# Splitting 192 channels as 128 and twice 64, and moving ACT's copies a piece behind their matmuls, in a two-layer vision-Mamba kernel

## The chip, the cores and the metric

The kernel runs on one core of a Trainium2 chip. The metric is the device time of one execution in microseconds, the median of three runs. A core has the engines PE (matmuls), DVE (vector), ACT (scalar, activation tables), POOL (GpSimd) and SP, which here issues the DMAs. [...]

## The reference, cut to what matters

The input is 8 images of 64 x 64 pixels with 192 channels. Two layers follow each other. Per image, with L = 4096 pixels:

```python
# layer 0
xl, z = split(x @ W_in.T)                      # 192 -> 2 * 384
xc = silu(depthwise3x3(xl) + conv_b)
# two orders of the pixels (rows, columns), each with its own B, C (32 states) and dt (6 heads)
h = exp(dt * A) * h + (dt * x_t) B_t           # per head: 64 x 32
y = h C_t + D * x_t                            # the two orders are added
out = x + (y * silu(z)) @ W_out.T              # 384 -> 192
x1 = out + silu(out @ W1.T + b1) @ W2.T + b2   # 192 -> 768 -> 192
# layer 1, on x1
left  = relu(conv1x1(relu(bn(conv3x3(relu(bn(conv3x3(bn(x1[:96]))))))))
right = layernorm, projection to 192, depthwise conv, silu, then
        delta = softplus(dt_proj(dts) + bias)  # four directions, 192 channels
        h = exp(delta * A) * h + delta * u * B # 16 states per channel
        y = h C + D * u
        layernorm, times silu(z), projection to 96
out = shuffle(left, right) + x1
```

All of it is in f32 except the spreading of delta * u, which is done in three bf16 terms.

## The kernel before

**The spine** is `selective_scan`, layer 1's recurrence. Its work for 8 images is cut into 3072 units q, 384 per image: a unit has 8 channels times 16 states on 128 partitions and 1024 pixels. A tile is 16 units; it takes its delta and delta * u from `prepare`. Per unit, `fetch` brings delta by a DMA (4 units ahead), ACT's `decay` makes exp(delta * A) of it (L1322), PE's `spread` (L1330) lays delta * u over the states into one of two PSUM tiles dB, DVE multiplies by B (`weigh`, L1345) and scans (L1352), POOL multiplies by C (L1356), ACT's `carry_on` takes the last column (L1362, L1363), and every fourth unit PE's `gather` (L1374) sums over the states of four units into a PSUM tile acc, which ACT copies out (L1378). The gather runs two units behind the scan.

**The side work** is everything else: generators, one after the other, that the class `Beside` runs in pieces. For image b + 1 these are layer 0's `conv0` (projection to 384 and depthwise convolution), `ssd` (layer 0's recurrence, in 32 chunks of 128 pixels) and `mlp0` (gate, projection, and the two-layer product), then layer 1's `conv_branch` (with `scan_sums` aside) and `scan_outputs` of an earlier image, and `scan_inputs` and `transposed`, which make the next image's u. For the first image they run alone, before the scan begins, and in this first run the yields of each generator are added up as its cost.

The order of the work is set by this bookkeeping, not by a scheduler: all instructions are recorded in program order (`pin`). Each unit has two half slots. In a half slot the order is: the next piece of a running gather; then `Beside.half()`; then a piece of `prepare`; and in the first half `carry_on` of the unit before, `spread` of the next, and the scan. `half()` adds a rate to a credit and runs side pieces until the yields that they give have used it up; a `yield None` ends the half at once:

```python
        self.rate = (own + sum(self.costs.get(gen.__name__, 40.0) for gen in self.stages)) / halves
...
        self.credit = min(self.credit, self.rate) + self.rate
        while self.credit > 0.0 and self.stages:
            for cost in self.stages[0]:
                if cost is None:
                    return
                self.credit -= cost
                if self.credit <= 0.0:
                    return
```

`own` (465 before) stands for the scan's own PE work, which takes credit by `beside.spend`. In the last but one tile of an image, 23 units ahead of its end, `beside.finish()` runs at once whatever side work is left; then the next image's u is loaded and the next stages are started. `conv_branch` counts 190 and `scan_outputs` 78 as cost.

**Layer 0's matmuls before.** The 192 input channels lie on 96 partitions, twice. A product from 192 channels is two matmuls of 96 rows that add up: L362 in conv0 (512 columns), L693 (gate) and L739 (expand) in mlp0 (256 columns). A product to 192 channels makes two halves of 96 output partitions: L726 (project) and L757 (contract), 256 columns. mlp0 goes through 16 blocks of 256 pixels by stages that overlap by `in_turn` (L682 is the addition of the two orders on POOL). One f32 matmul shows as two rows in the trace, and L-numbers of a helper's matmul are those of the helper's line.

**ssd's chunk.** `in_turn` runs fetch, decays, weigh, outputs and store, a chunk apart, the oldest first. `decays` loads X by four DMAs, transposes B and C (L545), which ACT copies (bc, L549), and makes the decay factors M: PE's L555 and L556 into ps_d, ACT's exp (L557). `weigh` has POOL's xw (L571), dtx (L577) and the decayed state Hm (L579). `outputs` has the state sums on PE (L589), DVE's additions to Hm (L595) and Hn (L611), POOL's Hn (L597), and the outputs (L605, L620, L626) with DVE's additions (L615, L633). `store` writes y by four DMAs.

Outside dB's two, PSUM has four tiles of 512 columns during the scan; `cx.one` hands them out for all side work, for the gather and for `prepare`. `prepare` makes delta's raw values by two matmuls of 12 rows, one per half of the pixels (L1262), each followed by ACT's work on its half.

Of the kernel before, what the change touches and what calls it, by code (L numbers as in the profile page):

```python
# [41 lines left out]
NXP = 4 * NS + 2 * RK  # L42
# [66 lines left out]
def setup(cx, cp, dp, p0, p1):  # L109
# [42 lines left out]
    k["b2"] = const(p0["b2"].rearrange("(a p) -> p a", p=CH), [CH, 2], "b2")  # L152
# [34 lines left out]
    nc.sync.dma_start(out=k["dtw"][4 * NS : NXP], in_=p1["dtw"].rearrange("g r t m -> r g t m"))  # L187
# [138 lines left out]

def conv0(cx, x):
# [3 lines left out]
    with cx.pool("cw0") as wp, cx.pool("v0", 2) as vp:  # L331
        w_in = wp.tile([CH, 2, INNER0], F32, tag="w_in", name="w_in")
        pin(nc.sync.dma_start(out=w_in, in_=k["p0_w_in"].rearrange("(a p) m -> p a m", p=CH)[:, :, :INNER0]))
# [11 lines left out]
        first = vp.tile([CH, 2, R2 * WW], F32, tag="xt", name="first")[:, :, :WW]  # L345
        pin(nc.sync.dma_start(out=first, in_=x[:, 0:WW].rearrange("(a p) l -> p a l", p=CH)))
        xts, xcs = {}, {}

        def load(p):

            n = min(R2, HH - 1 - p * R2)
            xts[p] = vp.tile([CH, 2, R2 * WW], F32, tag="xt", name="xt")
            at = (p * R2 + 1) * WW
            pin(nc.sync.dma_start(
                out=xts[p][:, :, : n * WW], in_=x[:, at : at + n * WW].rearrange("(a p) l -> p a l", p=CH)
            ))

        def rows_in(j, src, n, at):

            ps = cx.one("ps_in")  # L360
            for a in range(2):
                pin(nc.tensor.matmul(  # L362
                    ps[:, : n * WW], lhsT=w_in[:, a, j * 128 : (j + 1) * 128], rhs=src[:, a, :], start=a == 0, stop=a == 1
                ))
            pin(nc.scalar.copy(
                pads[j][:, at : at + n, 1 : 1 + WW], ps[:, : n * WW].rearrange("p (h w) -> p h w", w=WW)
            ))

        def project(p, j):
            pad = pads[j]  # L370
            if p == 0:
                rows_in(j, first, 1, 1)
            else:
                pin(nc.gpsimd.tensor_copy(pad[:, 0:2, :], pad[:, R2 : R2 + 2, :]))
            for b in range(2):
                n = min(RB, HH - 1 - p * R2 - b * RB)
                if n < RB:
                    pin(nc.gpsimd.memset(pad[:, R2 + 1, :], 0.0))
                rows_in(j, xts[p][:, :, b * RB * WW : (b * RB + n) * WW], n, 2 + b * RB)
                yield 2.4  # L380
# [58 lines left out]
def ssd(cx):  # L439
# [15 lines left out]
    with cx.pool("g0", 2) as gp, cx.pool("s0", 2) as sp:  # L455
# [79 lines left out]
        def decays(c):  # L535
# [3 lines left out]
            for d in range(2):  # L539
                for i, (at, dims) in enumerate(token_rows(k["xrows"], d, c, 1)):  # L540
                    src = bass.AP(k["xrows"].tensor, k["xrows"].offset + at, [dims[0], [1, INNER0]])
                    pin(nc.sync.dma_start(out=flat(X[chunks[i], d]), in_=src))
            ps = cx.one("ps_t")
            for i in range(2):
                pin(nc.tensor.transpose(  # L545
                    ps[: 2 * N0, i * Q : (i + 1) * Q], both[:, c % GC, i].rearrange("p d n -> p (d n)"), k["ident"]
                ))
            bc = sp.tile([2 * N0, 2, Q], F32, tag="bc", name="bc")
            pin(nc.scalar.copy(bc.rearrange("p i t -> p (i t)"), ps[: 2 * N0, : 2 * Q]))  # L549
            yield 0.6  # L550
            M = sp.tile([128, 2, NH, S], F32, tag="M", name="M")
            R = st[c].pop("R")
            for d in range(2):
# [3 lines left out]
                pin(nc.scalar.activation(flat(M[:, d]), ps, AF.Exp))  # L557
                yield 1.0
            st[c].update(X=X, bc=bc, M=M)

        def weigh(c):
# [7 lines left out]
            heads = "p d h c -> p (d h) c"  # L569
            xw = sp.tile([128, 2, NH, HP], F32, tag="xw", name="xw", bufs=1)  # L570
# [7 lines left out]
            Hm = sp.tile([2 * N0, NH, HP], F32, tag="H", name="Hm", bufs=4)  # L578
            pin(nc.gpsimd.tensor_mul(Hm, state[c], bcast(over[:, 0, c % GC, :], 2, HP)))  # L579
            st[c].update(dtx=dtx, xw=xw, Hm=Hm)  # L580

        def outputs(c):
# [26 lines left out]
            yield None  # L609
            ps = pss[1].rearrange("p (h c) -> p h c", c=HP)  # L610
            pin(nc.vector.tensor_add(Hn, ps, Hn))  # L611
            yo = sp.tile([128, 2, NH, HP], F32, tag="yo", name="yo")
# [23 lines left out]
        def store(c):  # L636
            yo = st.pop(c)["yo"]
            yield 0.0
            for d in range(2):
                y = k["yrows"][d]  # L640
                for i, (at, dims) in enumerate(token_rows(y, d, c, 1)):
                    dst = bass.AP(y.tensor, y.offset + at, [dims[0], [1, INNER0]])
                    pin(nc.sync.dma_start(out=dst, in_=flat(yo[chunks[i], d])))
            yield 0.0
# [4 lines left out]
def mlp0(cx, x, x1):  # L649

    nc, pin, k = cx.nc, cx.pin, cx.k
    NF, T = HID // 128, 256
    with cx.pool("mw0") as wp, cx.pool("m0", 2) as mp:
        def weight(n, shape, src):
            t = wp.tile(shape, F32, tag=n, name=n)
            pin(nc.sync.dma_start(out=t, in_=src))
            return t

        w_z = weight("w_z", [CH, 2, INNER0], k["p0_w_in"].rearrange("(a p) m -> p a m", p=CH)[:, :, INNER0:])
        w_out = weight("w_out", [128, NJ, C], k["p0_w_out"].rearrange("(j p) m -> p j m", p=128))  # L660
        w1 = weight("w1", [CH, 2, HID], k["p0_w1"].rearrange("(a p) m -> p a m", p=CH))
        w2 = weight("w2", [128, NF, C], k["p0_w2"].rearrange("(f p) m -> p f m", p=128))
        gT = wp.tile([128, NJ, T], F32, tag="gT", name="gT")
        h1 = wp.tile([128, NF, T], F32, tag="h1", name="h1")
        tiles = (slice(0, 2), slice(2, 3))
        st = {}

        def cols(i):
            return slice(i * T, (i + 1) * T)

        def load(i):
            st[i] = {}
            for d, bufs in ((0, 3), (1, 1)):
                t = st[i]["y", d] = mp.tile([128, 2, INNER0], F32, tag=f"y{d}", name=f"y{d}", bufs=bufs)
                pin(nc.sync.dma_start(out=t, in_=k["yrows"][d][cols(i)].rearrange("(q p) c -> p q c", p=128)))
            xt = st[i]["xt"] = mp.tile([CH, 2, T], F32, tag="xt", name="xt", bufs=4)
            pin(nc.sync.dma_start(out=xt, in_=x[:, cols(i)].rearrange("(a p) l -> p a l", p=CH)))
            yield 0.0

        def add(i):  # L680
            y0, y1 = st[i]["y", 0], st[i].pop(("y", 1))
            pin(nc.gpsimd.tensor_add(y0, y0, y1))  # L682
            yield 0.0

        def gate(i):
            xt = st[i]["xt"]
            zs = st[i]["zs"] = mp.tile([128, NJ, T], F32, tag="zs", name="zs", bufs=1)
            for js in tiles:
                ps = cx.one("ps_z")
                n = (js.stop - js.start) * T  # L690
                for j in range(js.start, js.stop):
                    for a in range(2):
                        pin(nc.tensor.matmul(  # L693
                            ps[:, (j - js.start) * T : (j - js.start + 1) * T], lhsT=w_z[:, a, j * 128 : (j + 1) * 128],
                            rhs=xt[:, a, :], start=a == 0, stop=a == 1,
                        ))
# [910 lines left out]
```

## Time and profile before

| | us |
|---|---|
| median of three runs | 18009.72 (18006.15 to 18019.03) |
| the profiled execution | 17986.38 |
| its span, first to last instruction | 17984.4 |
| PE, DVE, POOL, ACT busy | 14375.7, 12309.3, 12008.5, 10711.9 |
| mean granted PE clock | 0.815 of full |
| from the first scan to the last one's end | 980.8 to 17754.5 |

The span begins with 981 us in which the first image's layer 0 runs alone. Then come eight images of the scan, about 2190 us each in the steady state (less for the first and the last, which have less side work), and about 230 us of the last image's sums and outputs. The page's groups give each line's busy time, the mean of one instruction, and the time for which its engine stood idle before it with what ended that. A group's busy time counts rows that overlap once. The table of stretches gives, for chosen stretches of time, each engine's busy time, its instructions, the granted PE clock and the share of the DMA engines; the table for a line gives the same for that line's instructions alone.

### The profile page before, as it was taken

To read this page: it belongs to the slowest core of one execution; us is meant where nothing else is said; L and a number is where in the kernel's file an instruction comes from. 1 tells how busy PE (TensorE), PEld (TensorE's weight loads), DVE (VectorE), ACT (ScalarE), POOL (GpSimd) and SP (SyncE) were. 2 spreads that over 40 slices of the span, in tenths; PEclk is the share of its full clock that TensorE was granted. 3 is DMA by queue.
4 is the path that set the end of the run, shared out by engine and by line. 5 is a ranking of instruction groups with operands and counts; after the bars stand their busy time and mean duration, and the time that the engine had idled before them with its cause. 6 is when DMAs were issued, how large, how long until landed. Compare 5 with 4: busy or idle time off the path is not lost. (4 is left out here: it accounts for less than half of the span.)

```text
span 17984.4 us, 224777 instructions
## 1 busy us (share of the span) xinstructions
PE 14375.7 (80%) x76904; PEld 5676.6 (32%) x76904; DVE 12309.3 (68%) x9392; ACT 10711.9 (60%) x18482; POOL 12008.5 (67%) x6437
## 2 busy tenths in 40 slices
PE   8977788788877888778878788787888778868776
PEld 4623332343223431334313342233422334211111
DVE  2167787776667766677657775677766777667785
ACT  2464676466664756647566485664756557555654
POOL 3168776776668755687657875678755786657774
PEclk9987788789787887878878798787987779877676
DMA  3277777777677776777767777777776777677785
GB/s 85 75 201 177 189 190 202 168 193 199 170 195 174 192 194 164 196 176 201 186 170 188 176 199 185 184 188 178 197 183 178 184 183 198 180 194 190 184 196 143
DMA packets 1600969, 3238.93 MB, mean 180 GB/s; under 512 B 391580, under 2 KB 869396, under 8 KB 1596244
## 3 DMA queue, kind: packets, MB, share of 16 engines
q1 hardware_dynamic: 1599828, 3224.55, 71.2%
q8 instruction: 614, 10.06, 0.3%
q14 instruction: 527, 4.32, 0.1%
HBM read 2545.63 MB, written 678.18 MB: 179 GB/s over the span
## 5 line engine op out<-in xcount | busy, mean ns | idle before, releaser
L1356 POOL TENSOR_TENSOR h<-h,bc 128x1023 f32<-128x1023 f32 x3072 | 7223.5, 2354 | 3926.6 <-DVE h L1352 3412.2
L1352 DVE TENSOR_TENSOR_SCAN h<-dA,carry,dB 128x1024 f32<-128x1024 f32 x3072 | 7198.8, 2343 | 624.0 <-ACT dA L1322 188.7
L1345 DVE TENSOR_TENSOR dB<-dB,bc 128x1024 f32<-128x1024 f32 x3072 | 3741.5, 1218 | 2996.7 <-PE dB L1330 2948.1
L1322 ACT ACTIVATE dA<-dA,neg_a 128x1024 f32<-128x1024 f32 x3072 | 3486.8, 1135 | 797.5 <-DMA dA<-dld 795.3
L1374 PE MATMUL acc<-h,gather 128*32 128x512 f32 x12288 | 2479.9, 758 | 525.7 <-POOL h L1356 203.2
L1378 ACT COPY y<-acc 128x512 f32<-128x512 f32 x1536 | 886.5, 577 | 1908.7 <-PE acc L1374 1891.4
L1330 PE MATMUL dB<-dus,spread 24*128 24x512 bf16 x6144 | 1418.8, 430 | 365.3 <-DVE h L1352 283.8
L795 PE MATMUL ps_c<-p,conv_w 96*96 96x512 f32 x2304 | 1250.9, 670 | 120.5 <-ACT p L816 105.8
L1330 PEld LDWEIGHTS <-spread 24*128 24x128 bf16 x6144 | 317.6, 93 | 2607.9 <-issue 1700.3
L620 PE MATMUL ps_y<-dtx,M 64*64 64x64 f32 x12288 | 824.3, 267 | 393.5 <-DVE Hn L611 387.1
L1363 ACT ACTIVATE h<-h,bc 128x1 f32<-128x1 f32 x3072 | 905.1, 295 | 163.3 <-ACT carry L1362 3.8
L620 PEld LDWEIGHTS ps_y<-dtx,M 64*64 64x64 f32 x12288 | 691.6, 177 | 572.8 <-issue 349.5
L1374 PEld LDWEIGHTS acc<-h,gather 128*32 128x32 f32 x12288 | 321.2, 119 | 1690.8 <-issue 836.4
L319 PE MATMUL ps_cv<-pad,diag 64*64 64x512 f32 x6912 | 849.9, 611 | 5.6 <-ACT xo L399 2.8
L1276 POOL TENSOR_TENSOR w<-w,e 128x1024 f32<-128x1024 f32 x192 | 452.6, 2357 | 510.7 <-ACT carry L1362 423.7
L757 PE MATMUL ps_m<-h,w 128*96 128x256 f32 x3072 | 750.1, 392 | 30.2 <-DVE gT L715 20.4
L739 PE MATMUL ps_h<-o,w 96*128 96x256 f32 x3072 | 749.3, 397 | 4.3 <-ACT zs L697 1.7
L1362 ACT COPY carry<-h 128x1 f32<-128x1 f32 x3072 | 575.4, 187 | 250.9 <-DVE h L1352 248.1
L739 PEld LDWEIGHTS ps_h<-o,w 96*128 96x128 f32 x3072 | 585.6, 196 | 174.6 <-issue 62.3
L795 PEld LDWEIGHTS ps_c<-p,conv_w 96*96 96x96 f32 x2304 | 367.5, 177 | 814.8 <-issue 703.3
L555 PE MATMUL ps_d<-R,after 128*128 128x384 f32 x1024 | 554.8, 631 | 84.6 <-DVE M L575 36.8
L106 ACT ACT_TABLE_LOAD x481 | 617.1, 1283 | 8.2
(244 smaller groups left out, 22124.1 us busy)
## 6 DMA issues: line engine op xcount, KB each, us to landing
dA<-dld SPq DMA_DIRECT2D x3072, 512.0 KB
dud<-terms SPq DMA_DIRECT2D x192, 768.0 KB
dus<-dud SPq DMA_DIRECT2D x2304, 64.0 KB
bc<-bcd SPq DMA_DIRECT2D x256, 512.0 KB
X<-xrows SPq DMA_DIRECT2D x1024, 96.0 KB
yrows<-yo SPq DMA_DIRECT2D x1024, 96.0 KB
y<-yrows SPq DMA_DIRECT2D x256, 384.0 KB
u<-u SPq DMA_DIRECT2D x192, 512.0 KB
```

The lines of the kernel that those rows point to most:

```text
L319: pin(nc.tensor.matmul(ps[64 * b : 64 * (b + 1)].rearrange("p (h w) -> p h w", w=WW), lhsT=diag[:, t, :], rhs=pad[64 * i : 64 * (i + 1), b ...
L620: pin(nc.tensor.matmul(psy[d][here, h * HP : (h + 1) * HP], lhsT=M[here, d, h, :], rhs=dtx[here, d, h, :], start=True, stop=d == 1,))
L739: pin(nc.tensor.matmul(ps[:, n * T : (n + 1) * T], lhsT=w1[:, a, (f + n) * 128 : (f + n + 1) * 128], rhs=o[:, a, :], start=a == 0, stop=a ...
L795: pin(nc.tensor.matmul(ps.rearrange("p (h w) -> p h w", w=WW), lhsT=w[:, t, :], rhs=pad[:, dy : dy + RB, dx : dx + WW], start=t == 0, stop ...
L1322: pin(nc.scalar.activation(dAs[q], dAs[q], AF.Exp, scale=k["neg_a"][:, steps[m][1], t, i : i + 1]))
L1330: pin(nc.tensor.matmul(dBs[q][:, half, :], lhsT=k["spread"][at : at + 3 * UD, :], rhs=du_of[n][at : at + 3 * UD, i // 2, :], start=True, s ...
L1345: pin(nc.vector.tensor_mul(dBs[q], dBs[q], of(q)[0]))
L1352: pin(nc.vector.tensor_tensor_scan(order(h, g), order(dA, g), order(dB, g), carry, ALU.mult, ALU.add))
L1356: pin(nc.gpsimd.tensor_mul(h[:, rest], h[:, rest], C_[:, rest]))
L1363: pin(nc.scalar.activation(end, end, AF.Identity, scale=C_[:, last : last + 1]))
L1374: pin(nc.tensor.matmul(ps[32 * v : 32 * (v + 1)], lhsT=k["gather"], rhs=hs[q - 3 + v][:, here], start=True, stop=True))
L1378: pin(nc.scalar.copy(y[:, here], ps))
```

## The change

The 192 channels are laid as 128 partitions, and the other 64 twice: for two blocks of pixels at once, block 0's 64 on the lower and block 1's on the upper partitions. `product` takes two blocks: one matmul of 128 rows for each, then one of 64 rows for each. mlp0 goes through 8 pairs of blocks and has its stages written out in order; products to 192 channels become `narrow`, with 128 outputs over 512 columns and then 64 outputs for each block in two halves of the columns of PE. The small dt product gets its weights and rows twice (from partitions 64 and 96), so that the two halves of the pixels take different rows of PE, and both are issued together. In ssd the loads and stores of the first order become one DMA each; ACT's copy of bc and the exps stand one piece later; Hm is first among POOL's three; the addition to Hn comes ahead of the `yield None`. The gather's copy comes after its `yield`, at the next half slot. Yields and `own` are set anew.

```diff
-NXP = 4 * NS + 2 * RK
+DTS = (64, 96)
+NXP = DTS[1] + 2 * RK
...
+def product(cx, outs, weight, cols, xa, xbs):
+    nc, pin = cx.nc, cx.pin
+    for out, x in zip(outs, xa):
+        pin(nc.tensor.matmul(out, lhsT=weight[0][:, cols], rhs=x, start=True, stop=False))
+    for b, (out, x) in enumerate(zip(outs, xbs)):
+        pin(nc.tensor.matmul(out, lhsT=weight[1][64 * b : 64 * (b + 1), cols], rhs=x, start=False, stop=True))
...
 # conv0, project
-            for b in range(2):
-                rows_in(j, xts[p][:, :, b * RB * WW : (b * RB + n) * WW], n, 2 + b * RB)
-                yield 2.4
+            pss = [cx.one("ps_in") for b in range(2)]
+            product(
+                cx, [ps[:, : n * WW] for ps, n in zip(pss, ns)], w_in, cols,
+                [xa[:, b * RB * WW : (b * RB + n) * WW] for b, n in enumerate(ns)],
+                [xb[64 * b : 64 * (b + 1), : n * WW] for b, n in enumerate(ns)],
+            )
+            yield 1.8
+            for b, n in enumerate(ns):
+                rows_in(j, pss[b], n, 2 + b * RB)
+            yield 1.8
...
 # ssd, decays
+            yield 0.6
             bc = sp.tile([2 * N0, 2, Q], F32, tag="bc", name="bc")
             pin(nc.scalar.copy(bc.rearrange("p i t -> p (i t)"), ps[: 2 * N0, : 2 * Q]))
-            yield 0.6
...
-                pin(nc.scalar.activation(flat(M[:, d]), ps, AF.Exp))
+                if d == 1:
+                    pin(nc.scalar.activation(flat(M[:, 0]), ahead, AF.Exp))
                 yield 1.0
+                ahead = ps
+            pin(nc.scalar.activation(flat(M[:, 1]), ahead, AF.Exp))
...
 # ssd, weigh: ahead of xw; before, it stood behind dtx
+            Hm = sp.tile([2 * N0, NH, HP], F32, tag="H", name="Hm", bufs=4)
+            pin(nc.gpsimd.tensor_mul(Hm, state[c], bcast(over[:, 0, c % GC, :], 2, HP)))
...
 # ssd, outputs
             yield 0.9
-            yield None
             ps = pss[1].rearrange("p (h c) -> p h c", c=HP)
             pin(nc.vector.tensor_add(Hn, ps, Hn))
+            yield None
...
 # mlp0
+        def narrow(weight, n, rhs, psa, psb):
+            for f in range(n):
+                pin(nc.tensor.matmul(psa, lhsT=weight[:, f, 0:128], rhs=rhs(f), start=f == 0, stop=f == n - 1))
+                yield 1.2
+            for f in range(n):
+                for b, low in enumerate(lows):
+                    pin(nc.tensor.matmul(
+                        psb[low, :T], lhsT=weight[:, f, 128:C], rhs=rhs(f)[:, b, :], start=f == 0, stop=f == n - 1
+                    ))
+                yield 0.6
...
+        def expand(i):
+            for f in range(0, NF, 2):
+                pss = [cx.one("ps_h") for b in range(2)]
+                for n in range(2):
+                    at = slice(n * T, (n + 1) * T)
+                    cols = slice((f + n) * 128, (f + n + 1) * 128)
+                    product(cx, [ps[:, at] for ps in pss], w1, cols, *both(*os[i]))
+                    if n == 0:
+                        yield 1.8
+                for n in range(2):
+                    for b, ps in enumerate(pss):
+                        pin(nc.scalar.activation(
+                            h1[:, f + n, b, :], ps[:, n * T : (n + 1) * T], AF.Silu, bias=k["b1"][:, f + n : f + n + 1]
                         ))
...
-        yield from in_turn(range(L // T), load, add, gate, turn, project, expand, contract, store)
+        load_x(0)
+        load_y(0)
+        for i in range(NI + 1):
+            if i < NI:
+                yield from gate(i)
+                add(i)
+            if i > 0:
+                yield from expand(i - 1)
+            if i < NI:
+                yield from turn(i)
+                if i + 1 < NI:
+                    load_x(i + 1)
+                    load_y(i + 1)
+            if i > 0:
+                yield from contract(i - 1)
+            if i < NI:
+                yield from project(i)
...
 # selective_scan, prepare
-            for i, here in enumerate(halves):
-                ps = cx.one("ps_dt")
-                pin(nc.tensor.matmul(
-                    ps, lhsT=k["dtw"][4 * NS : NXP, g, t, :], rhs=rows[4 * NS : NXP, here], start=True, stop=True
-                ))
-                beside.spend(1.2)
+            pss = [cx.one("ps_dt") for here in halves]
+            for ps, at, here in zip(pss, DTS, halves):
+                took = slice(at, at + 2 * RK)
+                pin(nc.tensor.matmul(ps, lhsT=k["dtw"][took, g, t, :], rhs=rows[took, here], start=True, stop=True))
+            beside.spend(1.2)
+            for i, (ps, here) in enumerate(zip(pss, halves)):
                 yield 1 + i
...
 # selective_scan, gather
                 beside.spend(1.6)
+                yield
                 pin(nc.scalar.copy(y[:, here], ps))
-                yield
...
-        beside.spread_over(halves, 465.0)
+        beside.spread_over(halves, 450.0)
```

The sums of yields per image become 237 for conv0 (251 before) and 283 for mlp0 (347); those of ssd, scan_inputs and transposed stay (about 245, 125 and 12).

## The prediction

> **What bounds the kernel now.** I read the page's busy times first, then cut one image of the steady state (the sixth) into its six side stages in the table of stretches, then asked each stage for its waits, and last read single stretches of the timeline.
>
> ```profile
> PE 14375.7 (80%) x76904; PEld 5676.6 (32%) x76904; DVE 12309.3 (68%) x9392; ACT 10711.9 (60%) x18482; POOL 12008.5 (67%) x6437
> ...
> L1345 DVE TENSOR_TENSOR dB<-dB,bc 128x1024 f32<-128x1024 f32 x3072 | 3741.5, 1218 | 2996.7 <-PE dB L1330 2948.1
> ```
>
> No engine is full. DVE's scan chain is the spine (1.22 + 2.34 us per unit, 3072 units), and its main wait is for PE's spread matmul, which stands behind side work in PE's order.
>
> ```profile
> 11587.50:11949.60 362.10, 310.04 (x1952) 120.12 (x1952) 267.49 (x152) 252.56 (x463) 243.54 (x120) 0.86 0.79 199
> 11949.60:12526.10 576.50, 428.64 (x3966) 196.17 (x3967) 436.12 (x438) 253.07 (x502) 479.01 (x303) 0.75 0.73 174
> 12526.10:13031.90 505.80, 438.79 (x1912) 245.66 (x1912) 400.40 (x288) 412.20 (x656) 368.87 (x168) 0.92 0.77 195
> 13031.90:13377.80 345.90, 287.59 (x773) 79.15 (x773) 191.06 (x108) 153.67 (x279) 189.00 (x98) 0.87 0.73 189
> 13377.80:13539.50 161.70, 128.00 (x295) 28.88 (x295) 108.70 (x89) 123.61 (x191) 104.66 (x55) 0.75 0.67 174
> 13539.50:13776.40 236.90, 178.98 (x716) 41.98 (x717) 131.90 (x85) 142.97 (x219) 115.48 (x60) 0.69 0.64 169
> ```
>
> The rows are conv0, ssd, mlp0, conv_branch, scan_outputs, and scan_inputs with transposed; the columns after the length are PE, PEld, DVE, ACT, POOL. PE is the fullest in conv0 (86%) and mlp0 (87%), POOL in ssd (83%). The same table for L1352 counts scans: 76, 91, 104, 54, 24, 35 units. The waits of the ssd stretch:
>
> ```profile
> ACT y L1378 <- PE acc L1374: 102.6, 29, 9.4
> ...
> PE ps_y L620 <- DVE Hn L611: 58.7, 25, 4.0
> DVE Hm L595 <- POOL Hm L579: 52.4, 14, 9.2
> ACT M L557 <- PE ps_d L556: 51.4, 56, 2.8
> ...
> ACT bc L549 <- PE ps_t L545: 43.9, 13, 7.1
> ```
>
> At an image's end something else is to be seen, first DVE, then ACT:
>
> ```profile
> 13732.82 2.35 DVE L1352 TENSOR_TENSOR_SCAN h<-dA,carry,dB 128x1024 f32<-128x1024 f32 x1
> 13786.85 1.23 DVE L1345 TENSOR_TENSOR dB<-dB,bc 128x1024 f32<-128x1024 f32 x1 [51.69 <-PE dB L1330]
> ```
> ```profile
> 13743.15 14.62 ACT L994 COPY part<-whole 128x1024 f32<-128x1024 f32 x8 [11.02 <-DMA whole<-u]
> ```
>
> All eight copies of transposed run in one block: its pieces had not had their turn when finish() ran out the rest, and the scan stands for 52 us. Five of seven boundaries show 48 to 52 us; the one after image 0, where the copies were spread, 23.9; the last, with no conv0 behind it, 22.6.
>
> [...]
>
> ```profile
> 218.84 1.70 PE L408 MATMUL ps_p<-xp,xc 64*128 64x140 f32 x24
> 220.47 0.88 PE L398 MATMUL ps_x<-ident,xc 128*128 128x128 f32 x6
> 221.28 1.70 PE L408 MATMUL ps_p<-xp,xc 64*128 64x140 f32 x24
> ```
> ```profile
> 544.78 4.26 PE L739 MATMUL ps_h<-o,w 96*128 96x256 f32 x19
> 548.88 2.32 PE L726 MATMUL ps_o<-gT,w_out 128*96 128x256 f32 x10
> ```
>
> A row of 256 columns takes (548.88 - 544.78) / 19 = 0.216 us; an f32 matmul is two rows, 0.432 us (512 columns: 0.864). By columns, 24 rows of 140 would need 2.83 us in line; they take 1.63, start to start. In pairs they need 1.42, so entering the 64-row mode costs 0.21. Six rows of 128 need 0.65 of 0.81 (221.28 - 220.47), so leaving costs 0.16. An excursion is 0.37 us. [...]
>
> **The change, part by part,** per steady image, at full clock first.
>
> (a) Channels 128 + 2 x 64. A product of two blocks was 4 matmuls and is 2 plus a concurrent pair. At 256 columns that is 1.73 against 1.30 + 0.37: 0.06 saved, almost nothing. At 512 (conv0) 3.46 against 2.96: 0.49 x 12 = 6 us. project: 12 x 0.432 = 5.18 against 3 x 0.864 + 3 x 0.432 + 0.37 = 4.26; contract: 10.37 against 8.15. For mlp0: 72 x 0.06 + 8 x 0.92 + 8 x 2.22 = 29 us. In the built order some excursions fall on a switch that the spread or gather costs anyway: mode changes in mlp0 rise by 111 per image, not by 2 x 88; at 0.185 each that is 21 us against 61 of streaming saved, so 40, or 44 at the clock of 0.92. Bounds: 20 (every switch at twice the price) to 60 (free).
>
> (b) The dt product. L1262 is 68.7 us of PE per image in the table of its line (96 rows[...]). Two now run in two row groups, as the spread pair does: half, 34 us. `rows` grows from 76 to 108 partitions at the same columns: nothing.
>
> (c) Pacing. The yields of mlp0 fall from 347 to 283 per image, of conv0 from 251 to 237, own from 465 to 450, the spends of the dt product by 29. By the built order mlp0 gets 89 units (104), conv0 75 (76), ssd 91 (91), conv_branch 56 (54), the rest 73 (59), and transposed's copies stand in units 357 to 361 of 384 instead of all in 361.
>
> mlp0: PE 438.8 - 44 - 15 units x 1.33 (spread 0.42, gather 0.76, the rest dt and x projection) - 6 (dt) = 369. ACT loses 15 x 2.5 = 37 (L1322 1.14, L1362 and L1363 0.48, half a copy 0.29, prepare 0.58) and 25 table loads of 1.283 = 32 (197 fewer in the built order over 8 images): 343. DVE 341, POOL 321. All four keep their proportion to PE, so at PE's share of 86.8% mlp0 takes 425: -81. conv0: PE -6 / 0.86 - 7.5 (dt) - 1.3, at its share -18; its start issues 5 more DMAs on SP, 0.65 us each, ahead of the first matmul: +3. So -15. conv_branch: two units more of PE work against 3 us of dt: 0. The rest: 14 units more at 4.0 (3.56 of DVE and its gaps) = +56, the flush 52 -> 24 = -28: +28.
>
> (d) ssd. Hm goes ahead of xw and dtx on POOL, a half slot earlier (half of 6.3 us per unit) than a wait that lasts 3.7 us on average (52.4 / 14): about 40 go, if the Hn that it reads is there; its add on DVE moves up a half slot too, which also shortens PE's wait for Hn. What is late next is xw, by L579's 0.82 us, and PE's ps_s behind it: at most 26, I take 8. dtx is not moved past anything. ACT's copies behind: bc, M and y waited 198 us here, but ACT is 44% busy, and DVE hardly waited for it. 64 DMAs fewer on SP for X and yrows, 31 more elsewhere; SP is not what anyone waits for here. I take -35, bounds 0 and -75 (POOL's 479 us is a floor not far below).
>
> (e) gather's copies behind, everywhere. They free carry and decay, which stand behind the copy on ACT: DVE waited 128 + 189 us in all for these, 40 per image. I take -8; bounds +60 (rival 3) and -40.
>
> Sum per steady image: -81 - 15 + 0 + 28 - 35 - 8 = -111; six of them, the last without the 28 of the flush: -638. Image 0 (mlp0 118 to 105 units -70, conv0 -15, ssd -31, the rest 10 units +40, (e) -8): -84. Last image, DVE-bound: -10 of its dt. Before the scan starts, mlp0 alone is 269 us of which PE 262: streaming -61, 88 excursions +33, and ACT's silu between expand and contract, covered by a turn only, about +2 per block, +16: -12; conv0 -6, ssd -12: -30. In all -762: the span 17984 becomes 17222, the profiled execution 17986 becomes 17224. The median of the runs, 18010, lies 23 above the profiled one; I keep that: **17,250 us**.
>
> **Rivals.** (1) *The mode switches eat the packing.* For it: (a) leaves 0.06 us per product. Then mlp0 loses only its 15 units and dt: PE 412 / 0.868 = 475, -31; ssd and (e) nothing, conv0 -8; +28: -11 per image, in all, with nothing from the start, about 17,950. (2) *The stages close up further,* mlp0 at 92% (400 us; conv0 past its start, 13785 to 14110, has 91%), ssd at -60, (e) -20: -173 per image, about 16,850. [...] (3) *Slower: banks.* There are four PSUM banks for all side work and the gather. gather's bank is now held up to a half slot longer (2.9 us), products take two banks at once, narrow holds two for some seven halves (11.4 of yields at 1.6 a half). Each of 192 gather copies per image could hold up PE's next matmul. It decides from 111 / 192 = 0.58 us each; at 0.8 us, +43 per image, 18,350. [...] Against: the waits list for acc on an ACT copy in before is short (34.7 us for L1268, 31 times), and ACT has 19% slack even in mlp0. (4) *It does not do what it says:* the built order shows that it does, so what is left is that gains are given back, near 18,000.
>
> **Chances.** Forecast 0.67 (own range 17,050 to 17,500); (2) 0.14; (1) 0.11; (3) 0.05; (4) 0.03. About 0.2% is what a measurement of this kernel can tell from no change. The range takes in the unknown bounds of (a), (d) and (e) and the whole of (2), and leaves out (1), (3) and (4): 16,850 to 17,700. (1) ends near the bound, so some of it counts as same: faster 0.89, same 0.05, slower 0.06.
>
> **What would show it.** mlp0 at 410 to 440 us for 89 units with PE busy near 370; L1262's rows overlapping in pairs and half its busy time; no eight-fold block of transposed's copies and no DVE gap of 50 us; the Hm wait under 15 us per image in ssd; bc, M and y gone from ACT's longest waits. Wrong would be: PE waiting for banks behind ACT or DVE in mlp0, PE busy in mlp0 above 400, ssd unchanged at 576.

## The result, and the profile after

The changed kernel takes 17,881 us (median of five runs, 17,818 to 17,928), 0.9929 of the time before, 95% interval 0.9904 to 0.9954. The forecast was 17,250. The sign was right, the size six times too large. The profiled execution, the slowest of the five, has a span of 17,925.8 us, against 17,984.4 before.

The page's busy times and DVE's costliest wait:

```profile
PE 13953.2 (78%) x75752; PEld 4910.9 (27%) x75752; DVE 12239.1 (68%) x9264; ACT 10435.9 (58%) x18285; POOL 12013.0 (67%) x6437
...
L1418 DVE TENSOR_TENSOR dB<-dB,bc 128x1024 f32<-128x1024 f32 x3072 | 3741.6, 1218 | 3133.2 <-PE dB L1403 3126.0
```

PE has 423 us less to do, and DVE waits 178 us longer for the spread than before (3126.0 against 2948.1). The same image in the table of stretches, with the same columns (conv0, ssd, mlp0, conv_branch, scan_outputs, scan_inputs with transposed):

```profile
11570.10:11941.70 371.60, 292.26 (x1943) 109.21 (x1943) 263.43 (x150) 250.66 (x460) 236.64 (x118) 0.86 0.76 190
11941.70:12528.50 586.80, 432.05 (x3971) 193.77 (x3971) 434.22 (x438) 253.05 (x501) 483.19 (x304) 0.74 0.68 170
12528.50:12981.70 453.20, 366.79 (x1682) 154.83 (x1682) 342.61 (x242) 350.64 (x576) 320.17 (x146) 0.91 0.77 196
12981.70:13336.70 355.00, 300.27 (x776) 81.41 (x777) 198.05 (x112) 157.55 (x286) 194.68 (x100) 0.86 0.73 187
13336.70:13500.50 163.80, 138.73 (x291) 30.03 (x291) 110.95 (x90) 120.64 (x188) 105.97 (x56) 0.67 0.67 172
13500.50:13758.70 258.20, 191.05 (x808) 44.43 (x809) 177.23 (x112) 174.63 (x278) 160.46 (x79) 0.76 0.78 199
```

The image takes 2188.6 us; before, 2188.9. (The profiled execution lies 46 us above the median of its kernel, so some 6 us of an image may be its own.) PE's busy time in mlp0 is what was forecast (366.8, forecast 369), but the stage ends at 453 and not at 425; conv0, ssd and conv_branch each take 9 to 10 us more, and the last row 21 more. What the run gained lies outside the steady images: the first scan starts at 934.9 instead of 980.8, and the last image takes 1667 instead of 1730 us, while the first takes 2015 instead of 1951. The waits of ssd in this image, first before the change (lines beside those that the prediction showed), then after it (us in total, times, longest):

```profile
ACT carry L1362 <- DVE h L1352: 20.9, 12, 2.7
...
DVE Hn L611 <- POOL Hn L597: 17.9, 13, 2.5
...
DVE Hm L595 <- PE ps_s L589: 9.6, 7, 1.7
```
```profile
ACT bc L591 <- PE ps_t L586: 86.5, 23, 11.0
...
DVE Hn L654 <- POOL Hn L641: 66.9, 26, 5.6
ACT carry L1435 <- DVE h L1425: 55.8, 21, 8.4
...
ACT y L1452 <- PE acc L1447: 45.2, 21, 6.2
DVE Hm L639 <- PE ps_s L633: 41.7, 19, 3.6
ACT M L599 <- PE ps_d L597: 41.7, 30, 2.8
PE ps_y L664 <- DVE Hn L654: 38.3, 15, 4.4
```

The wait for POOL's Hm (52.4) is gone; in its place the addition to Hn waits 66.9 instead of 17.9 for POOL, and Hm's own addition 41.7 instead of 9.6 for PE. ACT's waits for bc, M and y were to go; with the 28.0 of the second exp (M, L602) they come to 201 us, against 198 before. At the end of the image the timeline of DVE has

```profile
13769.53 1.23 DVE L1418 TENSOR_TENSOR dB<-dB,bc 128x1024 f32<-128x1024 f32 x1 [33.56 <-PE dB L1403]
13867.82 1.23 DVE L1418 TENSOR_TENSOR dB<-dB,bc 128x1024 f32<-128x1024 f32 x1 [14.40 <-PE dB L1403]
```

so one stall of 33.6 and a new one of 14.4, where 51.7 stood. transposed's eight copies still come within 24 us (13715.8 to 13739.5).

### The profile page after: what moved, and what is told of

It reads as the page before. It is cut to its first block, busy times and chain, and to the rows that moved or that the text cites. A ratio compares the mean times of both kernels' runs of the same rounds, so it can differ in the third digit from the quotient of the medians.

```text
span 17925.8 us, 221564 instructions
## 1 busy us (share of the span) xinstructions
PE 13953.2 (78%) x75752; PEld 4910.9 (27%) x75752; DVE 12239.1 (68%) x9264; ACT 10435.9 (58%) x18285; POOL 12013.0 (67%) x6437
## 5 line engine op out<-in xcount | busy, mean ns | idle before, releaser
L1418 DVE TENSOR_TENSOR dB<-dB,bc 128x1024 f32<-128x1024 f32 x3072 | 3741.6, 1218 | 3133.2 <-PE dB L1403 3126.0
L1403 PE MATMUL dB<-dus,spread 24*128 24x512 bf16 x6144 | 1364.2, 432 | 437.9 <-DVE h L1425 340.0
L868 PE MATMUL ps_c<-p,conv_w 96*96 96x512 f32 x2304 | 1294.9, 690 | 116.3 <-ACT p L889 105.3
L664 PE MATMUL ps_y<-dtx,M 64*64 64x64 f32 x12288 | 758.1, 253 | 298.5 <-DVE Hn L654 291.1
L664 PEld LDWEIGHTS ps_y<-dtx,M 64*64 64x64 f32 x12288 | 635.8, 165 | 491.1 <-issue 259.7
L596 PE MATMUL ps_d<-R,after 128*128 128x384 f32 x1024 | 627.3, 706 | 111.1 <-DVE M L621 54.1
L350 PE MATMUL ps_h<-oa,w1a 128*128 128x256 f32 x1536 | 483.0, 438 | 159.1 <-ACT h L810 90.0
L591 ACT COPY bc<-ps_t 64x256 f32<-64x256 f32 x256 | 93.4, 365 | 728.6 <-PE ps_t L586 726.3
L779 PE MATMUL ps_m<-h,w 128*128 128x512 f32 x768 | 436.2, 710 | 78.3 <-DVE gT L774 36.8
L654 DVE TENSOR_TENSOR Hn<-ps_s,Hn 64x384 f32<-64x384 f32 x256 | 139.9, 546 | 518.8 <-POOL Hn L641 510.2
```

The costliest lines, as they stand in the source:

```text
L664: pin(nc.tensor.matmul(psy[d][here, h * HP : (h + 1) * HP], lhsT=M[here, d, h, :], rhs=dtx[here, d, h, :], start=True, stop=d == 1,))
L868: pin(nc.tensor.matmul(ps.rearrange("p (h w) -> p h w", w=WW), lhsT=w[:, t, :], rhs=pad[:, dy : dy + RB, dx : dx + WW], start=t == 0, stop ...
L1403: pin(nc.tensor.matmul(dBs[q][:, half, :], lhsT=k["spread"][at : at + 3 * UD, :], rhs=du_of[n][at : at + 3 * UD, i // 2, :], start=True, s ...
L1418: pin(nc.vector.tensor_mul(dBs[q], dBs[q], of(q)[0]))
```

## The experiments

All times in one table. The ratio is to the kernel before, run on the same chip. The medians come from several chips, on which the kernel before itself took 17,981 to 18,010 us, so rows are compared by their ratios; a difference of ratios is given in us of 18,010. The columns from "start" on are from the trace: the time of the first scan, then the mean lengths of five steady stages of each kind, each from its first matmul to the first of the next (in us), and the mean period of images 2 to 6.

| kernel | median us | ratio (95%) | start | conv0 | ssd | mlp0 | branch | outputs | inputs | image |
|---|---|---|---|---|---|---|---|---|---|---|
| before | 18,010 | 1 | 981 | 370 | 576 | 508 | 334 | 166 | 235 | 2188 |
| the change | 17,881 | 0.9929 (0.9904–0.9954) | 935 | 371 | 586 | 456 | 353 | 160 | 260 | 2186 |
| packing_alone | 17,892 | 0.9944 (0.9931–0.9956) | 941 | 379 | 567 | 460 | 346 | 165 | 264 | 2181 |
| moves_alone | 17,974 | 0.9991 (0.9982–1.0000) | 974 | 368 | 594 | 510 | 330 | 167 | 223 | 2188 |
| d_undone | 17,795 | 0.9900 (0.9886–0.9915) | 940 | 371 | 573 | 454 | 345 | 161 | 258 | 2160 |
| e_gather_first | 17,998 | 1.0003 (0.9994–1.0013) | 932 | 375 | 586 | 458 | 346 | 163 | 261 | 2188 |
| hn_undone | 17,676 | 0.9836 (0.9822–0.9850) | 932 | 373 | 558 | 454 | 345 | 158 | 259 | 2145 |
| acts_undone | 17,888 | 0.9948 (0.9936–0.9961) | 938 | 371 | 589 | 454 | 347 | 158 | 256 | 2174 |
| only_hm | 17,703 | 0.9839 (0.9819–0.9860) | 935 | 373 | 561 | 456 | 350 | 158 | 258 | 2155 |
| good_moves_alone | 17,798 | 0.9885 (0.9864–0.9905) | 978 | 369 | 570 | 508 | 330 | 166 | 221 | 2162 |
| before_less_pe | 17,939 | 0.9978 (0.9969–0.9987) | 934 | 370 | 575 | 509 | 333 | 168 | 229 | 2181 |
| before_paced | 17,945 | 0.9974 (0.9959–0.9989) | 980 | 386 | 578 | 443 | 345 | 168 | 257 | 2177 |
| paced_good_moves | 17,797 | 0.9892 (0.9876–0.9907) | 976 | 379 | 565 | 440 | 349 | 170 | 260 | 2161 |
| one_bank_narrow | 17,896 | 0.9955 (0.9943–0.9967) | 935 | 372 | 585 | 458 | 349 | 158 | 262 | 2182 |
| behind3 | 17,834 | 0.9916 (0.9896–0.9935) | 938 | 379 | 560 | 481 | 338 | 159 | 255 | 2174 |
| xo3 | 17,625 | 0.9800 (0.9780–0.9819) | 934 | 362 | 561 | 456 | 346 | 159 | 257 | 2140 |
| spread_first | 17,538 | 0.9741 (0.9721–0.9760) | 939 | 360 | 559 | 450 | 340 | 162 | 257 | 2129 |
| denser_mlp0 | 17,670 | 0.9820 (0.9798–0.9842) | 939 | 365 | 588 | 425 | 343 | 172 | 254 | 2146 |

### Packing or moves

My theory after the result was that PE's freed time is not what the steady image waits for. The rival was that the moves (d) and (e) took back what the packing gained. Four kernels test this: (d) and (e) are both undone, made without the rest, or undone one at a time. Their edits are those of the change or the same reversed. packing_alone has neither (d) nor (e):

> The changed kernel with ACT's copies, Hm and the additions to Hn where they stood before, and the gather's copy ahead of its yield; packing, dt pair and new yields stay. Theory (the time PE gained is not what the steady image waits for; the moves matter little): 17,880 to 17,950, mlp0 near 453 us with PE busy near 367. Rival (the moves in ssd and the gather took back what the packing gained): 17,250 to 17,500, with ssd at 575 us or less, conv0 at 350 and mlp0 near 425.

moves_alone has only these two, on the kernel before:

> The kernel before with only ACT's copies, Hm, the addition to Hn and the gather's copy moved; channels, dt product and yields as before. Theory: the moves matter little, within 60 us of before (18,010), ssd 575 to 587 us. Rival (the moves took back what the packing gained): 18,300 to 18,600, PE waiting for banks or for Hn in every stage.

d_undone and e_gather_first undo one each:

> The changed kernel with the order inside ssd (bc, the exps, Hm, Hn) as before; the gather's copy stays behind its yield. Theory: within 40 us of the changed kernel (17,880), ssd 577 to 590 us. Rival (early Hn turns the wait for POOL's Hm into one for POOL's Hn and for the copy bc): ssd back to 570 or below, 17,750 to 17,800.

> The changed kernel with the gather's copy ahead of its yield again. Theory: within 40 us of the changed kernel (17,880). Rival (the copy that comes later holds a bank of four and so PE, the prediction's slower case): 17,500 to 17,700, and fewer waits of PE for DVE and ACT in conv0, branch and mlp0.

The theory held for packing_alone and for the time of moves_alone (its ssd, 594, was longer than said). It fell for the other two, which lie 86 and 117 us from the changed kernel by the medians, where it allowed 40. The rival's case came true for d_undone alone (17,795; ssd 573). Packing, dt pair and new yields together give 0.0056 (101 us of 18,010), of which 40 are the earlier start; the steady image gains 7 us. So the packing gain that the rival supposed was never there. But the moves do matter, each with its own sign: the gather's copy behind its yield gains 0.0044 (79 us) without (d) and 0.0074 (133 us) with it, where I had expected 56 us and the rival a loss; and (d), forecast to gain, costs 0.0029 with the late gather (52 us; by the medians 86; the two intervals overlap) and 0.0059 (106 us) without it.

### Which line of ssd

Theory: the addition to Hn half a slot earlier is the harmful line. DVE comes to it before POOL has made Hn (it waits 66.9 us in the sixth image's ssd, 17.9 before), and what stands behind it on DVE comes later (ACT's wait for the scan's h is 55.8 us, 20.9 before). Rival: ACT's late copies.

```diff
 # hn_undone: on the changed kernel
             yield 0.9
+            yield None
             ps = pss[1].rearrange("p (h c) -> p h c", c=HP)
             pin(nc.vector.tensor_add(Hn, ps, Hn))
-            yield None
```

> The changed kernel with only the addition to Hn back behind its pause; Hm first and ACT's copies late stay. Theory (the early addition is the harmful move: DVE waits 67 us per ssd for POOL's Hn, 18 before): ssd 565 to 575 us, 17,780 to 17,820, as good as with all of ssd's order undone (17,795). Rival (ACT's late copies are the harmful move): ssd stays at 585, 17,860 to 17,900.

acts_undone puts bc and the exps straight behind their matmuls and keeps the early addition; only_hm does the same on top of hn_undone, so that of (d) only Hm's place is left; good_moves_alone is the kernel before with (d) and (e) but without the early addition.

> The changed kernel with only ACT's copies of ssd (bc and the exps) straight behind their matmuls again; Hm first and the early addition to Hn stay. Theory (the early addition is the harmful move): 17,860 to 17,900, ssd still at 585 us. Rival (ACT's late copies are the harmful move): ssd 565 to 575, 17,780 to 17,820.

> The changed kernel with the addition to Hn as before and ACT's copies of ssd straight behind their matmuls again; Hm stays first. Theory (Hm's place is what gains, since DVE waits for POOL's Hm and not for ACT): 17,670 to 17,710, ssd 560 us. Rival (ACT's copies gain it): 17,770 to 17,810, ssd 570 to 575.

> The kernel before with the moves of ACT's copies, of Hm and of the gather's copy, and without the early addition to Hn; channels, dt product and yields as before. Theory (these moves help by themselves, some 25 us per image): 17,760 to 17,830, ssd 560 us, which leaves 80 to 150 us to packing and pacing. Rival (the moves only help once PE has time to spare): above 17,920, ssd above 570.

The place of one `yield None` is worth 0.9929 to 0.9836, 167 us (205 by the medians, which are of different chips), more than the 60 to 100 that the theory said; ssd goes from 586 to 558. The pair moves_alone and good_moves_alone shows it on the old layout, 0.9991 to 0.9885, 191 us; good_moves_alone met its expected time, with ssd at 570 and not 560. ssd's waits in hn_undone:

```profile
PE ps_y L664 <- DVE Hn L655: 49.8, 22, 5.0
DVE Hm L639 <- PE ps_s L633: 49.4, 21, 4.5
...
DVE Hn L655 <- POOL Hn L641: 28.8, 15, 3.8
...
ACT carry L1435 <- DVE h L1425: 26.6, 16, 4.1
```

The wait for POOL's Hn falls from 66.9 to 28.8, and with it ACT's wait for the scan's h, which stands behind on DVE, from 55.8 to 26.6. The place of ACT's copies does nothing that can be measured: acts_undone is at 0.9948 against 0.9929 of the change, only_hm at 0.9839 against 0.9836 of hn_undone, and the intervals overlap. Hm's place alone gains 0.9900 (d_undone) to 0.9839 (only_hm), 110 us.

### What PE's time is worth

before_less_pe takes from the old mlp0 the time that packing was to give, and nothing else. It leaves out three of the six terms of contract's sums:

```diff
                 for f in range(NF):
-                    pin(nc.tensor.matmul(
+                    if f in (0, 4, 5):
+                        pin(nc.tensor.matmul(
```

> The kernel before with half of contract's matmuls left out (three of six terms of each sum; the outputs are then those of three terms), all yields as before: some 40 us less of PE per image in mlp0, the saving that the prediction gave to the packing, without second banks, switches of mode or new pacing. The prediction's step (PE's share of mlp0 stays at 86.8%): -46 us per image, mlp0 at 460, about 17,660. Theory (with the pacing given, the units' time in mlp0 is set by the orders of the engines and hardly by PE's busy time): mlp0 above 490, 17,880 to 18,000.

Per image 96 matmuls of 0.432, 41.5 us, are gone; mlp0 stays at 509 us, with the 104 units that it had. The run gains 0.0022 (40 us), and the first scan, ahead of which mlp0 runs alone, starts 47 us earlier, which is of that size; from the first scan to the last one's end the profiled execution takes 16,788 us, against 16,774 before. mlp0 of the sixth image, in the table of stretches (505.80 and 438.79 before):

```profile
12495.00:12997.20 502.20, 419.17 (x1720) 219.73 (x1720) 399.50 (x288) 411.83 (x656) 368.32 (x168) 0.87 0.75 197
```

In this stretch, three groups of the kernel before (busy, mean; idle before, by releaser)

```profile
L757 PE MATMUL ps_m<-h,w 128*96 128x256 f32 x384 | 95.6, 396 | 3.9 <-DVE gT L715 3.2 <-ACT h L744 0.7
L739 PE MATMUL ps_h<-o,w 96*128 96x256 f32 x384 | 92.3, 391 | 0.3 <-DVE o L764 0.3
L1374 PE MATMUL acc<-h,gather 128*32 128x512 f32 x408 | 78.7, 675 | 23.1 <-POOL h L1356 13.0 <-ACT h L1363 4.1 <-ACT dl L1268 2.3
```

become these:

```profile
L739 PE MATMUL ps_h<-o,w 96*128 96x256 f32 x384 | 100.1, 416 | 0.1
L1375 PE MATMUL acc<-h,gather 128*32 128x512 f32 x408 | 88.5, 743 | 40.6 <-POOL h L1357 21.0 <-ACT h L1364 8.5 <-ACT h L744 5.2
L758 PE MATMUL ps_m<-h,w 128*96 128x256 f32 x192 | 57.3, 431 | 5.5 <-DVE gT L715 3.5 <-ACT h L744 2.0
```

contract loses 38 us of PE. 18 come back as longer rows of expand and the gather (0.391 to 0.416 us, 0.675 to 0.743), the granted clock of the stage being 0.87 instead of 0.92, and 17 more lie in longer waits of the gather.

The second kernel keeps the work and changes the yields alone:

```diff
 # before_paced, on the kernel before: mlp0's yields times 283/347, conv0's as shown
-                yield 2.4
+                yield 2.1
...
-                beside.spend(1.2)
+                beside.spend(0.6)
                 yield 1 + i
...
-        beside.spread_over(halves, 465.0)
+        beside.spread_over(halves, 450.0)
```

> The kernel before with only the yields of the change: mlp0's scaled by 283/347, conv0's 2.4 to 2.1, the dt product's spends halved, own 450; all work as before, 41 us of PE more per mlp0 than in the changed kernel. Theory (the number of units sets a stage's time, PE's work hardly): mlp0 at 450 to 470 us with 89 units, the inputs stage at 255 to 265, in all 17,950 to 18,030. Rival (PE's work counts; the packing made the shorter mlp0 possible): mlp0 at 480 to 500 us, in all 18,080 to 18,300.

paced_good_moves adds the good moves. It differs from hn_undone by the dt pair and by packing with what came along: mlp0's stages in a written-out order, other blocks and table loads, 89 units in mlp0 instead of 90, and in ssd one DMA where there were two.

> The kernel before with the new pacing and all moves but the early addition to Hn, so the changed kernel with Hn as before (17,676) without packing and dt pair. Theory (PE's time hardly counts once the scan runs; what packing gains is the start, where nothing else runs, some 45 us): 17,700 to 17,760, mlp0 at 445 us or less. Rival (packing is worth what its PE time says, 78 us per image): above 18,000.

mlp0 takes 443 and 440 us with 90 units, below what either case said for before_paced: the new yields alone shorten it more than the whole change does (456). The row of before_paced for mlp0 of the sixth image:

```profile
12522.00:12961.80 439.80, 398.01 (x1832) 238.58 (x1832) 353.20 (x260) 371.04 (x592) 323.88 (x148) 0.94 0.79 203
```

PE is 90% busy there, ACT 84%. In the changed kernel PE has 31 us less and the stage takes 13 more. From paced_good_moves to hn_undone, so by the packing, the dt pair and what came along, the run gains 0.0056, 101 us, 43 of them at the start (976 to 932). The theory had put it near 45, the rival above 320: more than the first, far from the second. The steady image gains 16 us, where PE has 27 us less in mlp0 (means of 398.8 and 371.5), 19 less in conv0 (313.0 and 293.8), and the dt product besides.

In the changed mlp0 expand (L350) and contract (L779) now wait, over the whole run:

```profile
L350 PE MATMUL ps_h<-oa,w1a 128*128 128x256 f32 x1536 | 483.0, 438 | 159.1 <-ACT h L810 90.0 <-ACT gT L753 28.3 <-ACT y L1452 22.5
L779 PE MATMUL ps_m<-h,w 128*128 128x512 f32 x768 | 436.2, 710 | 78.3 <-DVE gT L774 36.8 <-ACT h L810 36.8 <-ACT y L1452 4.5
```

In before, the groups of L739 and L757 stood idle for 4.3 and 30.2 us, in paced_good_moves for 3.0 and 2.1. In mlp0 of the sixth image PE is idle for 41.8 us in before_paced and for 86.4 in the changed kernel; 33 of these 44.6 more stand ahead of the two groups. A product fills two banks at once, and by the program's order the next but one stands behind four silus of ACT (L810, for which expand's matmuls waited the 90.0 us above). one_bank_narrow tests the other place where two banks are held, project and contract: the 128 outputs are added out of their bank before that for the 64 is taken.

```diff
 # one_bank_narrow, in narrow
+            first(psa)
+            psb = cx.one(name)
             for f in range(n):
                 for b, low in enumerate(lows):
```

> The changed kernel, but project and contract hold one bank at a time: the 128 outputs are added out before the bank for the 64 is taken. Rival (banks: PE waits in mlp0 and in the gather for banks that are held): mlp0 from 455 to 430 us, 17,680 to 17,750. Theory (banks are a small part): mlp0 above 448, 17,840 to 17,890.

0.9955 against 0.9929 and mlp0 at 458: no gain. This speaks against the two banks held there, but does not rule them out, since the edit also puts the addition of the 128 outputs earlier in DVE's order, where the two additions to oa waited 62 us for PE over the run of the changed kernel. Expand's waits were not taken away by a run; with smaller groups ACT would, by my estimate, load its tables more often (1.283 us a load; before, 214 loads at L744 for 384 groups of silus; in the changed kernel, 157 at L810 for 192), so that kernel would have tested two things.

### What holds the spread

behind3 moves the gather one unit further behind the scan, on hn_undone.

```diff
-    AHEAD, BEHIND = 4, 2
+    AHEAD, BEHIND = 4, 3
...
-            h = hs[q] = np_.tile([128, LC], F32, tag="h", name="h", bufs=4 + BEHIND + 1)
+            h = hs[q] = np_.tile([128, LC], F32, tag="h", name="h", bufs=4 + BEHIND)
```

> The changed kernel with the addition to Hn as before (17,676), and the gather three units behind the scan instead of two, with the same seven buffers for h. Theory (the gather's wait for POOL's product h stands ahead of the next spread in PE's order and keeps PE from using its spare time): waits of PE for POOL h gone, 17,450 to 17,600. Rival (that wait is slack only): 17,640 to 17,720; above it if the scan now waits for a free h.

It lost 0.0080, 144 us. The gather's waits for POOL h fell from 698 us (492.1 of weight loads, 206.1 of matmuls) to 204, yet PE's wait for the scan and the scan's waits for ACT rose; hn_undone first, then behind3:

```profile
PE dB L1403 <- DVE h L1425: 358.0, 210, 9.7
...
DVE h L1425 <- ACT dA L1395: 194.3, 85, 8.6
DVE h L1425 <- ACT carry L1435: 100.7, 73, 4.7
```
```profile
PE dB L1403 <- DVE h L1425: 458.4, 276, 9.1
...
DVE h L1425 <- ACT dA L1395: 291.4, 139, 8.8
DVE h L1425 <- ACT carry L1435: 164.0, 54, 13.7
```

So taking most of the gather's wait for POOL away gained nothing, and this theory fell. Why the run got slower is not isolated: mlp0 took 481 us instead of 454, with 91 units instead of 89, and the scan waited only 41 us for a free h. xo3, on hn_undone, gives conv0's xo a third buffer, since ACT's wait for the store of xo had grown from 44.5 to 142.8 us.

```diff
-            xo = vp.tile([128, 2, INNER0], F32, tag="xo", name="xo")
+            xo = vp.tile([128, 2, INNER0], F32, tag="xo", name="xo", bufs=3)
```

> The changed kernel with the addition to Hn as before (17,676), and three buffers instead of two for conv0's xo (the first rows of the image lie in the buffers of xa and xb for that). Theory (ACT's copies to xo wait 22 us per image for the store of the copy before, and PE behind them): that wait gone, conv0 from 373 to 355 to 362 us, 17,560 to 17,610. Rival (the wait is covered by others): conv0 370 or more, 17,640 to 17,700.

conv0 goes from 373 to 362, the run from 0.9836 to 0.9800 (65 us), and this wait has left the list. spread_first, on xo3, moves the spread ahead of the side work:

```diff
                     next(gathering, None)
+                    if half == 0 and 0 < q and q + 1 < U:
+                        spread(q + 1)
                     beside.half()
...
-                        if q + 1 < U:
+                        if q == 0:
                             spread(q + 1)
                         scan(q)
```

> As with three buffers for xo (17,625), and the spread of the next unit ahead of the side work of the first half slot in PE's order, not behind it. Theory (DVE waits for the spread because of its place in PE's order): DVE's wait for PE dB falls from 3,020 to below 2,000 us, 17,200 to 17,500. Rival (PE then waits for the scan to free dB, and the side work behind it comes late): PE's wait for the scan rises above 1,000 us, 17,650 to 18,200.

DVE's wait for the spread, xo3 and then spread_first:

```profile
DVE dB L1421 <- PE dB L1406: 3022.1, 876, 108.2
```
```profile
DVE dB L1421 <- PE dB L1406: 2279.2, 698, 109.6
...
PE dB L1406 <- DVE h L1428: 587.6, 449, 9.9
```

743 us of this wait went, and 0.0059 of time (106 us; 87 by the medians) were won: 17,538, the best of all kernels here, 2.6% below the kernel before. Neither case had the size. The place of the spread in PE's order is one cause of the wait, but much of what it frees turns into others: PE's wait for the scan goes from 359.6 to 587.6, DVE's for dA from 176.6 to 334.5. denser_mlp0, on xo3, scales mlp0's yields by 0.85 again:

> As with three buffers for xo (17,625), and the yields of mlp0 scaled by 0.85 once more. Theory (mlp0's time follows its number of units, and the units that it loses come back in other stages at little less): mlp0 at 395 to 415 us with 77 units, in all 17,560 to 17,640. Rival (PE's packing can now be cashed in: mlp0 has PE time to spare, the others gain units that cost 3.6 us): 17,400 to 17,520.

mlp0 goes to 425 with 80 units, ssd to 588 with 96, and the run to 17,670 (0.9820 against 0.9800, intervals that just overlap). Neither case was right: units that leave mlp0 come back elsewhere at no less than they saved.

## Why the prediction was wrong, step by step

By the ratios, (a) to (c) gave 101 us, (e) 79, and (d) cost 52, in this order of adding them; the forecast had about 453, 56 and 253 of gain. For a steady image it had -111 us, and -2 was measured: ssd missed by 45, mlp0 by 29, conv_branch by 19, conv0 by 15, and the stages after them were 9 better. Two steps failed.

**"All four keep their proportion to PE, so at PE's share of 86.8% mlp0 takes 425"** is the first. The PE time itself was right (366.8, and 370.7 on the mean of six images), and so were the 89 units; the price of the mode switches was a part of that sum, an estimate from two stretches of the timeline (1.63 us where 1.42 were reckoned, 0.81 where 0.65), and was not measured by itself in mlp0; that a change of mode makes these differences was not shown. What failed is that the span follows PE at a constant share: less PE work at the same pacing moved mlp0 by nothing (before_less_pe), and new pacing at the same PE work moved it to 443, with a share of 90% (before_paced). The 52 us that mlp0 lost fit the 15 units and not the packing: before_paced lost 65 with 14 units fewer and no packing. Per unit, mlp0 takes 4.9 us in before (508 / 104), before_less_pe (509 / 104) and before_paced (443 / 90), and 5.1 in the changed kernel (456 / 89). The share is a result of the pacing and of the waits between engines (87%, 90% and, in the changed kernel, 81%), and not a limit. Rival (2), stages that close up, was wrong for the same reason.

**"I take -35, bounds 0 and -75"**, in (d), is the second. I gave one value to four moves of different sign. Hm's place did gain, 110 us in all, about 14 per image. For the addition to Hn I wrote "which also shortens PE's wait for Hn": it does (58.7 to 38.3), but what stands behind the addition on DVE waits with it (ACT's wait for the scan rose from 20.9 to 55.8, and fell to 26.6 in hn_undone), and POOL had one half slot less to make Hn (a wait of 66.9 us instead of 17.9). That is 28 us per ssd (586 against 558). The row for it could be read in the profile before, "DVE Hn L611 <- POOL Hn L597: 17.9, 13, 2.5": at 13 of 32 chunks the old, later place had no slack left, and half a slot of about 3 us was taken from all 32. The lower bound of 0 should have been a loss of up to 32 x 3 = 96 (an estimate). In (e) I reckoned with what stands behind a waiting copy on ACT; to this line of DVE I did not apply it.

The smaller terms. (b) The dt product fell from 558.4 to 343.0 us, 27 per image instead of 34. (c) outputs and inputs together took 19 us more for 14 units more (401 to 420), where 56 less the flush's 28 were forecast; in before_paced they are 24 us longer, so this is the pacing's. The flush fell from 51.7 to 33.6 us, and another stall of 14.4 stands behind it. conv_branch, costed at nothing, grew by 19 us, and by 11 in before_paced with the same work. (e) had the right sign and was larger than said: 10 to 17 us per image instead of 8. conv0's -15 became 0, although PE lost 18 us: ACT waited 142.8 us in all for the store of xo instead of 44.5 (xo3 gave 11 us per image back), and the new pacing alone made conv0 16 us longer in before_paced. The start was better than forecast, 46 instead of 30 us. The first image was forecast at -84 and took 64 more, the last at -10 and took 63 less; in before_paced these are +32 and -40, so a part is the pacing's. Together they gave +1, where -94 were forecast.

Rival (3), banks, found no support where it was tested (one_bank_narrow, within the limit named there, and the gather's late copy, which gains); expand's two banks stay open. Rival (4), that gains are given back, is what the steady images came to. Also open is why packing costs mlp0 13 to 14 us against the same pacing without it (456 and 443, 454 and 440): the waits of expand and contract are large enough (159.1 + 78.3 less 4.3 + 30.2 is 203 us, 25 per image), but no run isolates them. The written-out order of mlp0's stages and the lower granted clock (0.89 to 0.91, against 0.92 to 0.94 in before_paced) are further candidates that no run takes apart. What sets the 4.9 us per unit, where DVE's own work is 3.56, is answered only in part, by spread_first.

## What to carry to other kernels

An engine at 87% in a stage isn't the bound of the stage until removing its work moves the time (here 41.5 us of its matmuls were left out, and the stage took 509 us instead of 508). Take away that work in a throw-away kernel, or change the pacing alone, before a forecast is built on its share. A move that puts a waiting instruction earlier in its engine's order is to be priced by all that stands behind it (here ssd took 28 us more): look whether the producer is done at the new place, one half slot earlier, for every instance. And cost each moved line by itself, with its own sign: here one of them took back 191 of the 207 us that the other moves gained on the old layout, and 167 of 295 in the changed kernel.

## What the runs showed of the hardware

In mlp0, the granted PE clock was lower where PE was less busy with the same kinds of matmuls: over six images it is 0.89 to 0.92 before (PE 87% busy), 0.85 to 0.87 with half of contract left out (83%), and 0.92 to 0.94 in before_paced (90%). But the changed kernel, with other matmuls, has 0.89 to 0.91 at 81%, so the share alone does not say it. In the sixth image a row of expand took 0.391 us at 0.92 and 0.416 at 0.87; longer rows also raise the share, and these runs do not part the two. Of the 41.5 us of streaming left out in before_less_pe, PE's busy time shows 20 in the sixth image (438.8 to 419.2) and 17 on the mean of six (440.5 to 423.5), so part of the saving was given back.
